# The second feed-forward product of both layers by seven products of half blocks, with sums of activations on VectorE and GpSimd, and half sums of exp on GpSimd

## The chip, the cores and the metric

The kernel runs on one core of a Trainium2 chip. The metric is the device time of one execution in microseconds. TensorE (PE) multiplies, VectorE (DVE), ScalarE (ACT) and GpSimd (POOL) do elementwise work, and SyncE (SP) issues the DMAs. Each engine works through its own instructions in order and waits on semaphores for the others. Matrix products leave their results in PSUM, of which the kernel uses eight banks of 128 x 512 fp32; everything else stands in SBUF.

## The reference

The input is `x` of 64 graphs x 256 nodes x 256 features in fp32, and `adj`, 64 x 256 x 256 integers. Two layers follow each other. The first has two graph attention steps, whose softmax is taken over the nodes; the second has eight-head attention in which the softmax weight of a pair of nodes is multiplied by one of several value projections, by the value of `adj`. Both end in the same way, and the change is in the last but one line of each:

```python
# layer 0
h = _layernorm(residual + h, g_ln1, b_ln1)
residual2 = h
ff = jnp.matmul(jax.nn.relu(jnp.matmul(h, w_ff1) + b_ff1), w_ff2) + b_ff2
return _layernorm(residual2 + ff, g_ln2, b_ln2)
# layer 1
x = _ln(src + attn_out, g1, beta1)
ff = jax.nn.gelu(x @ W1 + b1, approximate=False) @ W2 + b2
return _ln(x + ff, g2, beta2)
```

The feed-forward goes from 256 features to 1024 and back to 256. All of it is fp32.

## The kernel before

Graphs are worked on in 32 pairs. `whole_way` takes one pair through graph attention (`gat_layers`), feed-forward, attention (`attention`) and a second feed-forward, and stores it. Rows of a pair are 512: two graphs (index `b`) of 256 nodes, in two blocks of 128 (index `j`).

**How the order is made.** The kernel plans its own order while it is built. Each pair is a Python generator that yields before each step of TensorE the events that the step waits for and the PSUM banks that it needs; other engines' work is handed to `put` with an engine, an assumed duration, a rank and the events that it waits for. `run` keeps up to four pairs going, and at each moment picks the engine whose next work could begin first by these assumed times. On TensorE it takes the oldest pair of those that have been ready for 0.3 us, and otherwise the one ready first; on the others the lowest rank. `keep_order` then fixes this order for each engine. Names such as "ff", "attention" and "gat" are held by one pair at a time. So the program is a fixed interleaving of up to four pairs on each engine; at run time an instruction that is not ready holds up all that stand behind it on its engine.

**First product.** `feed_forward` already computes the first product (L689) with seven products for eight blocks (class `Blocks`, steps p1 to p7, with sums of the input blocks by `Second.add`, L360, and sums of the weights by `block_sums`, L341, once at the start). Results are copied from PSUM by ScalarE (L695), added to by VectorE (L393), and activated by ScalarE (L701), in two slabs of two 128-column slices for each half of the 1024 hidden features. The hidden activations stand transposed: `f[m]` is 128 hidden features by 512 rows.

**Second product.** For each graph block `b` and each row block `j`, eight matmuls (L720) with `f[m]` as the stationary operand and 256 columns of `w2` as the moving one add up in half a PSUM bank: 32 of 128 x 128 x 256 for each feed-forward. When a bank is full, `add_rows` (L571, VectorE) adds it to the rows `y`, already scaled by `scaled` (L604, GpSimd, two operations of 128 x 512 a graph), and `layernorm` follows: statistics on VectorE (L581, L582), the root on GpSimd (L587 to L590), the normalisation on ScalarE (L594). The first bank's additions and layernorm run while the second bank is filled. Then `transposed` (L623, and DMAs of SP) turns the rows for the next stage, except for the few `hurried` stages at both ends, which TensorE transposes.

**Attention.** For each of two graphs and two groups of four heads, `scores` (L809) fills four banks, ScalarE takes exp of them (L818), VectorE multiplies by the mask (L822, two heads at a time, 128 x 1024) and adds the two halves of the node axis (L826, 128 x 512), and `products` multiplies exp and masked exp with the values (L840) and the half sums with ones (L843). VectorE divides (L852, L853), and `into_rows` projects (L862).

Of the kernel before, what the change touches and what calls it, by code (L numbers as in the profile page):

```python
# [18 lines left out]
P = 128  # L19
# [14 lines left out]
def two_layers(ctx: ExitStack, tc: tile.TileContext, t: dict, out: bass.AP, flag: bass.AP):  # L34
# [293 lines left out]
    def first_weights(name, wide=None):  # L328
# [7 lines left out]
        return s  # L336

    def block_sums(w, there):

        for to, a, b, op in ((4, 0, 2, ALU.subtract), (2, 2, 6, ALU.add), (3, 2, 0, ALU.subtract), (5, 1, 3, ALU.subtract)):  # L340
            there = put("vector", 0.6, lambda to=to, a=a, b=b, op=op: nc.vector.tensor_tensor(w[:, to], w[:, a], w[:, b], op),  # L341
                        there, rank=5)
        return there
# [322 lines left out]
    def feed_forward(y, normal, w, func, relieved, pair, stage):  # L666

        w1, b1, w2 = w
        onwards = stage == 0
        kind = "gelu" if func == AF.Gelu else None  # L670
        half = NF // 2
        f, evacuated = [None] * NF, [[None] * NF for _ in range(2)]
        if hurried(pair, stage):
            yield from transposed_on_tensor(y, normal, stage)
        second = Second(lambda c, h: normal["yT"].rearrange("p b a (c k i) -> p c k (b a) i", c=KC, k=2)[:, c, h],
                        "sums_yT", normal[0], normal[1])

        def slabs(t):

            rows, columns = [], (slice(0, N), slice(N, 2 * N))  # L680

            def begin():
                for c in range(2):
                    rows.append(work.tile([P, 2, 512], F32, name="ff", bufs=NF // 2))
                    for n in range(2):
                        f[t + n + c * half] = rows[c][:, n]

            def multiply(to, slab, a, b, **flags):
                nc.tensor.matmul(to, lhsT=w1[:, a, (t + slab) * P:(t + slab + 1) * P], rhs=b, **flags)  # L689

            def target(c, h):
                return rows[c][:, :, columns[h]]

            def copy(c, h, event):
                return put("scalar", 0.5, lambda: nc.scalar.activation(target(c, h), blocks.bank["x"], AF.Copy), event, rank=-1)  # L695

            def activate(c, h, event, of=None):
                for n in range(2):
                    m, to = t + n + c * half, rows[c][:, n, columns[h]]
                    source = to if of is None else of[:, n]  # L700
                    evacuated[h][m] = put("scalar", 0.4, lambda m=m, to=to, source=source: nc.scalar.activation(  # L701
                        to, source, func, bias=b1[:, m:m + 1]), event, rank=h - 1, function=kind,
                        frees=["bank"] * (n and of is not None))

            first = ([normal[0], normal[1], relieved, second.there[0]], ["ff"]) if t == 0 else ([], None)
            blocks = Blocks(second, first, begin, multiply, target, copy, lambda of, event: activate(1, 0, event, of), activate)
            return blocks

        a, b = slabs(0), slabs(2)
        for step in (a.p1, b.p1, a.p2, a.p6, b.p2, b.p6, a.p5, a.p7, b.p7, b.p5, a.p4, b.p4, a.p3):  # L710
            yield from step()
        order, end = (0, 1, 4, 5, 2, 3, 6, 7), b.p3
        for b in range(2):
            for j in range(2):
                for part in (order[:half], order[half:]):
                    yield [evacuated[j][m] for m in part] if b == 0 else [], None, j == 0 and part[0] == 0
                    if j == 0 and part[0] == 0:
                        p2 = bank()
                    for m in part:
                        nc.tensor.matmul(p2[:, j * D:(j + 1) * D], lhsT=f[m][:, (2 * j + b) * P:(2 * j + b + 1) * P],  # L720
                                         rhs=w2[:, m, :], start=m == 0, stop=m == NF - 1)
                    there = took(0.43 * len(part))
                    if b == j == 0 and part[0] == 0:
                        yield from end()
                        frees_at(clock["tensor"], ["yT", "sums_yT"])
            normal[b] = layernorm(y, b, add_rows(y, p2, b, there, normal["scaled", b]))
            if onwards:
                transposed(y, normal[b], normal, b, pair, 1)
            else:
                normal[b] = scaled(y, ln[3], b, normal[b])  # L730
        done_with("ff")


    def attention(y, normal, pair, all_adj):
# [66 lines left out]
        def scores(n):  # L801
# [22 lines left out]
            def halves(q):  # L824
                h[n][q] = work.tile([P, 2, N], F32, name="h", bufs=HQ)
                nc.vector.tensor_tensor(h[n][q], a[n][q][:, :, :N], a[n][q][:, :, N:], ALU.add)  # L826

            there = [put("scalar", 0.96, lambda q=q: weight(q), there, rank=0, function="exp", needs="a", frees=["bank"] * 2)
                     for q in range(HQ // 2)]
            masked.append([put("vector", 1.14, lambda q=q: mask(q), there[q], rank=0, needs="m") for q in range(HQ // 2)] +  # L830
                          [put("vector", 0.61, lambda q=q: halves(q), there[q], rank=0, needs="h") for q in range(HQ // 2)])

# [52 lines left out]
    def layernorm_weights(g, beta, more=None):  # L885
        rows, columns, passing = [on_all(g, D), on_all(beta, D)], None, None
        if more:
            passing = work.tile([P, 2, 512], F32, name="ff", bufs=NF // 2)[:, 0, :D]
            v = t[more]
            nc.sync.dma_start(passing, bass.AP(tensor=v.tensor, offset=v.offset, ap=[[0, P], [1, D]]))  # L890
            columns = column(g + "c"), column(beta + "c")
        return *rows, Event(), columns, passing
# [3 lines left out]
    ln = [layernorm_weights("L0_gnn_g_ln1", "L0_gnn_b_ln1", "L0_gnn_b_ff2")]  # L896
    ff0 = (first_weights("L0_gnn_w_ff1p"), column("L0_gnn_b_ff1"), weights("L0_gnn_w_ff2"))
    loaded[1] = load(1, 18.0)
# [11 lines left out]
    bv, bv0 = on_all("L1_gnn_bv1", D), column("L1_gnn_bv0")  # L910
    less_bv = work.tile([P, 2, 512], F32, name="ff", bufs=NF // 2)[:, 0, :D]
    nc.sync.dma_start(less_bv, bass.AP(tensor=t["L1_gnn_bv"].tensor, offset=t["L1_gnn_bv"].offset, ap=[[0, P], [1, D]]))
    wo = weights("L1_gnn_Wo")
    ln.append(layernorm_weights("L1_gnn_g1", "L1_gnn_beta1", "L1_gnn_b2"))
    ff1 = (first_weights("L1_gnn_W1p"), column("L1_gnn_b1"), weights("L1_gnn_W2"))
    ln.append(layernorm_weights("L1_gnn_g2", "L1_gnn_beta2"))
# [37 lines left out]
    def reliefs():  # L954

        def of_feed_forward(w, gb, event):
            there = with_beta(w[1], block(w[0]), FF // 2, gb[3][1])
            put("vector", 0.0, lambda: None, block_sums(w[0], with_g(lambda at: w[0][:, at], gb[3][0], [there])), event=event)

        yield [landed["ff0"]], None, 1  # L960
# [474 lines left out]
```

## Time and profile before

| | before |
|---|---|
| median of three runs | 3079.77 us (3076.63 to 3083.66) |
| profiled execution | 3077.64 us |
| its span, first to last instruction | 3075.9 us |
| mean granted clock of TensorE | 0.994 |
| PE, PEld, DVE, ACT, POOL busy | 3010.9, 2454.7, 2234.0, 1835.1, 1032.2 us |
| second product, L720, busy | 466.4 + 461.7 us, 4096 matmul records |
| first product, L689, busy | 316.1 + 312.4 + 128.9 + 127.8 us, 3584 records |
| half sums L826 on VectorE | 185.1 us, 256 instructions |
| additions L571 on VectorE | 173.0 us, 256 instructions |

PEld is TensorE's loading of the stationary operand, which overlaps the matmuls. One fp32 `nc.tensor.matmul` of the program stands in the profile as two loads and two matmuls. Busy time is the union of the instructions' spans on an engine; a matmul's recorded span is longer than its distance to the next, since they are pipelined. A row of a group names the line, engine, operation, output and inputs and their shapes, the count, the busy time, the mean of one in ns, and after the second bar the idle time just before these instructions and what ended it.

### The profile page before, as it was taken

Reading aid. Unit: us, or ns where it says so; the run is one execution under the profiler, and the core shown is the slowest. Engines: PE = TensorE matmul, PEld = TensorE weight load, DVE = VectorE, ACT = ScalarE, POOL = GpSimd, SP = SyncE. Lnnn points to the kernel's source line nnn. Section 1 sums busy time; section 2 is a strip of 40 time slices with the busy share of each in tenths; the row PEclk is TensorE's granted clock in tenths of the full one; section 3 lists DMA queues with packets and bytes.
Section 4 is the critical chain, followed back from the end, with each engine's and each line's share of the span. In section 5 each row is a group of like instructions: output and inputs, shape, how many; then the busy total and the mean of one; then the engine's idle time right before and its main releaser. Section 6 shows DMA issues by size and latency. Waiting matters only on the chain.

```text
span 3075.9 us, 52423 instructions
## 1 busy us (share of the span) xinstructions
PE 3010.9 (98%) x19154; PEld 2454.7 (80%) x19154; DVE 2234.0 (73%) x4411; ACT 1835.1 (60%) x4186; POOL 1032.2 (34%) x1542
## 2 busy tenths in 40 slices
PE   7999999999999999999999999999999999999998
PEld 6877778877878788887888778878788778788876
DVE  5787766788776867768677676686776777767774
ACT  4556665656665566565756566565666565655654
POOL 1332244232423243232352322533325333233223
PEclk8999999999999999999999999999999999999999
DMA  6211132102321122211231122311213211121000
GB/s 181 73 51 36 56 124 79 46 28 75 109 66 50 61 76 80 73 49 56 76 99 60 42 70 69 97 66 50 66 54 96 82 53 57 62 93 58 32 1 22
DMA packets 211865, 205.76 MB, mean 67 GB/s; under 512 B 22928, under 2 KB 171280, under 8 KB 211600
## 3 DMA queue, kind: packets, MB, share of 16 engines
q1 hardware_dynamic: 211184, 202.06, 20.5%
q8 instruction: 154, 2.52, 0.3%
q14 instruction: 111, 0.91, 0.1%
q10 hardware_dynamic: 416, 0.26, 0.0%
HBM read 137.51 MB, written 64.73 MB: 66 GB/s over the span
## 4 chain that ended last, share of the span: by engine, by line
PE 79%; DVE 10%; ACT 3%; DMA 3%; POOL 2%; issue 2%; SPq 1%; DVEq 0%; POOLq 0%; ACTq 0%
PE ps L720 24%; PE ps L689 20%; PE ps L840 6%; PE ps L764 6%; PE ps L769 6%; PE ps L809 4%; PE ps L545 3%; PE ps L529 3%; PE ps L862 2%; PE ps L843 2%; DVE e L502 2%; DVE x L571 2%; DVE st L581 1%; PE ps L558 1%; DMA home<-yb 1%
## 5 line engine op out<-in xcount | busy, mean ns | idle before, releaser
L587 POOL TENSOR_SCALAR less<-mv 128x2 f32<-128x2 f32 x256 | 65.4, 255 | 1596.6 <-DVE mv L582 1561.4
L594 ACT ACTIVATE x<-x,less,rstd 128x256 f32<-128x256 f32 x512 | 279.3, 594 | 418.8 <-POOL less L590 414.9
L720 PE MATMUL ps<-w_L_gnn_w_ff,ff 128*128 128x256 f32 x2048 | 466.4, 380 | 0.0
L720 PE MATMUL ps<-w_L_gnn_W,ff 128*128 128x256 f32 x2048 | 461.7, 380 | 0.9 <-ACT ff L701 0.9
L720 PEld LDWEIGHTS ps<-w_L_gnn_W,ff 128*128 128x128 f32 x2048 | 386.9, 190 | 61.0 <-issue 5.4
L720 PEld LDWEIGHTS ps<-w_L_gnn_w_ff,ff 128*128 128x128 f32 x2048 | 387.9, 190 | 57.2 <-issue 4.3
L393 DVE TENSOR_TENSOR ff<-ps,ff 128x512 f32<-128x512 f32 x384 | 261.1, 683 | 163.6 <-PE ps L689 127.1
L822 DVE TENSOR_TENSOR m<-a,adj 128x1024 f32<-128x1024 f32 x256 | 325.4, 1271 | 20.6 <-ACT a L818 20.5
L689 PE MATMUL ps<-yT,w_L_gnn_W1p 128*128 128x256 f32 x1280 | 316.1, 384 | 10.9 <-ACT ff L695 7.4
L689 PE MATMUL ps<-yT,w_L_gnn_w_ff1p 128*128 128x256 f32 x1280 | 312.4, 384 | 12.3 <-ACT ff L695 12.3
L818 ACT ACTIVATE a<-ps 128x512 f32<-128x512 f32 x512 | 266.8, 603 | 68.0 <-PE ps L809 67.1
L689 PEld LDWEIGHTS ps<-yT,w_L_gnn_W1p 128*128 128x128 f32 x1280 | 238.3, 190 | 61.8 <-ACT ff L695 17.9
L689 PEld LDWEIGHTS ps<-yT,w_L_gnn_w_ff1p 128*128 128x128 f32 x1280 | 241.3, 191 | 56.6 <-ACT ff L695 16.7
L571 DVE TENSOR_TENSOR x<-ps,x 128x512 f32<-128x512 f32 x256 | 173.0, 680 | 152.4 <-PE ps L720 120.3
L695 ACT ACTIVATE ff<-ps 128x512 f32<-128x512 f32 x384 | 221.1, 589 | 92.0 <-PE ps L689 90.1
L604 POOL TENSOR_TENSOR x<-x,b_L_gnn_g_ln 128x512 f32<-128x512 f32 x128 | 168.7, 1318 | 274.5 <-DVE yb L623 138.3
L852 DVE RECIPROCAL h<-ps 128x256 f32<-128x256 f32 x128 | 224.1, 1752 | 49.1 <-PE ps L843 48.9
L581 DVE BATCH_NORM_STATS2 st<-x 128x6 f32<-128x256 f32 x512 | 208.4, 407 | 4.7 <-issue 0.4
L701 ACT ACTIVATE ff<-ff,c_L_gnn_b_ff 128x256 f32<-128x256 f32 x384 | 174.4, 509 | 49.4 <-DVE ff L393 48.8
L604 POOL TENSOR_TENSOR x<-x,b_L_gnn_g 128x512 f32<-128x512 f32 x128 | 166.1, 1298 | 94.4 <-ACT x L594 74.8
L589 POOL TENSOR_TENSOR rstd<-rstd,mhalf 128x2 f32<-128x2 f32 x256 | 189.1, 739 | 21.3
L701 ACT ACTIVATE ff<-ff,c_L_gnn_b 128x256 f32<-128x256 f32 x384 | 172.0, 502 | 31.6 <-DVE ff L393 31.0
(138 smaller groups left out, 5499.8 us busy)
## 6 DMA issues: line engine op xcount, KB each, us to landing
home<-yb SPq DMA_DIRECT2D x182, 256.0 KB, 2.0
yT<-home SPq DMA_DIRECT2D x728, 64.0 KB, 2.0
rows<-row SPq DMA_DIRECT2D x60, 512.0 KB, 3.8
input<-in_xT SPq DMA_DIRECT2D x32, 512.0 KB, 4.0
x<-in_x SPq DMA_DIRECT2D x32, 512.0 KB, 4.1
out<-x SPq DMA_DIRECT2D x32, 512.0 KB, 2.9
input<-in_adjT SPq DMA_DIRECT2D x30, 512.0 KB, 4.1
v<-in_adjT SPq DMA_DIRECT2D x2, 512.0 KB, 6.6
```

The costliest lines, as they stand in the source:

```text
L393: nc.vector.tensor_tensor(self.target(c, h), self.bank[bank], self.target(c, h), ALU.add)
L571: return put("vector", 0.6, lambda: nc.vector.tensor_tensor(rows, p, rows, ALU.add), *events, frees=["bank"])
L581: nc.vector.bn_stats(st[:, j, :], rows[j])
L594: nc.scalar.activation(rows[j], rows[j], AF.Identity, bias=less[:, j:j + 1], scale=rstd[:, j:j + 1])
L604: nc.gpsimd.tensor_tensor(both, both, v.rearrange("p (k d) -> p k d", k=1).to_broadcast([P, 2, D]), op)
L689: nc.tensor.matmul(to, lhsT=w1[:, a, (t + slab) * P:(t + slab + 1) * P], rhs=b, **flags)
L695: return put("scalar", 0.5, lambda: nc.scalar.activation(target(c, h), blocks.bank["x"], AF.Copy), event, rank=-1)
L701: evacuated[h][m] = put("scalar", 0.4, lambda m=m, to=to, source=source: nc.scalar.activation(to, source, func, bias=b1[:, m:m + 1]), even ...
L720: nc.tensor.matmul(p2[:, j * D:(j + 1) * D], lhsT=f[m][:, (2 * j + b) * P:(2 * j + b + 1) * P], rhs=w2[:, m, :], start=m == 0, stop=m == N ...
L818: nc.scalar.activation(a[n][q][:, k], ps[2 * q + k], AF.Exp)
L822: nc.vector.tensor_tensor(m[n][q], a[n][q], adj, ALU.mult)
L852: there = put("vector", 1.68, lambda: nc.vector.reciprocal(s, po[:, N:]), there, rank=0)
```

## The change

**Second product.** The product of a feed-forward is taken as one of 2 x 2 blocks: activations in blocks of row half `j` by hidden half `c`, `w2` in blocks of hidden half by output half. Seven block products replace eight. `last_weights` loads the four blocks of `w2` with four DMAs, `last_sums` makes three sums and replaces one block by four subtractions on VectorE at the start, and the feed-forward waits for them (`w2_there`). The activation blocks stand in four tiles of 128 x 4 x 256, with a fifth for a sum (`ff`, five buffers of 4 KB a partition instead of four of the same size). The new generator `outwards` emits, for each of seven products, eight matmuls of 128 x 128 x 128, 56 in all. Three sums of activations t1, t2, t4 are made on VectorE (128 x 1024 each) and one, t3, on GpSimd. The products 1, 6, 7 add up in one half bank "x"; 2, 5, 3 in "z" and 4 in "w" of another bank. Between them VectorE adds quarters of the result to the rows: d1, d5, d6 and d3 of 128 x 256, d24 and d7 of 128 x 512. Product 5 starts "z" anew after d24 has read it and t1 is there; 6 waits for t2 and d1, 3 for t4 and d5, 7 for t3 and d6. The layernorms of both graphs wait for d24, d3 and d7.

**Half sums.** `halves` moves from VectorE to GpSimd, at rank 1 behind the layernorm's root and t3.

**Memory.** The program is built with a DMA scratch of 1024 bytes.

```diff
+    def last_weights(name):
+
+        s = const.tile([P, 7, NF // 2, P], F32, name="w_" + name)
+        for c, h, at in ((0, 0, 0), (1, 0, 1), (1, 1, 2), (0, 1, 3)):
+            nc.sync.dma_start(s[:, at], t[name][c * FF // 2:(c + 1) * FF // 2, h * P:(h + 1) * P].rearrange("(k p) d -> p k d", p=P))
+        return s
+
+    def last_sums(w, there, event):
+        for to, a, b in ((4, 3, 0), (5, 2, 4), (6, 2, 3), (3, 1, 5)):
+            there = put("vector", 0.6, lambda to=to, a=a, b=b: nc.vector.tensor_tensor(w[:, to], w[:, a], w[:, b], ALU.subtract),
+                        there, rank=5, event=event if to == 3 else None)
...
-        order, end = (0, 1, 4, 5, 2, 3, 6, 7), b.p3
-        for b in range(2):
-            for j in range(2):
-                for part in (order[:half], order[half:]):
-                    yield [evacuated[j][m] for m in part] if b == 0 else [], None, j == 0 and part[0] == 0
-                    if j == 0 and part[0] == 0:
-                        p2 = bank()
-                    for m in part:
-                        nc.tensor.matmul(p2[:, j * D:(j + 1) * D], lhsT=f[m][:, (2 * j + b) * P:(2 * j + b + 1) * P],
-                                         rhs=w2[:, m, :], start=m == 0, stop=m == NF - 1)
-                    there = took(0.43 * len(part))
-                    if b == j == 0 and part[0] == 0:
-                        yield from end()
-                        frees_at(clock["tensor"], ["yT", "sums_yT"])
-            normal[b] = layernorm(y, b, add_rows(y, p2, b, there, normal["scaled", b]))
+        yield from outwards(y, normal, f, evacuated, w2, w2_there, b.p3)
+        for g in range(2):
+            normal[g] = layernorm(y, g, *normal["added"])
...
+        def product(n, to, side, first=False):
+            for b in range(2):
+                for k in range(half):
+                    nc.tensor.matmul(banks[to][:, b], lhsT=side[:, k, b * P:(b + 1) * P], rhs=w2[:, n - 1, k],
+                                     start=first and b == k == 0, stop=True, skip_group_check=True)
+            return took(1.8)
+
+        def add(to, of, us, *events, frees=()):
+            return put("vector", us, lambda: nc.vector.tensor_tensor(to, of, to, ALU.add), *events,
+                       *(normal["scaled", b] for b in range(2)), rank=-1, frees=frees)
+
+        def combine(to, a, b, op, *events, engine="vector", us=1.14):
+            return put(engine, us, lambda: getattr(nc, engine).tensor_tensor(to, a, b, op), *events, rank=0)
...
+        yield [w2_there, *done(0, 0)], None, 1
+        x = banks["x"] = bank()[:, :D].rearrange("p (b d) -> p b d", b=2)
+        read1 = product(1, "x", a11, True)
+        d1 = add(quarter(0, 0), x, 0.34, read1)
+        yield from end()
+        frees_at(clock["tensor"], ["yT", "sums_yT"])
+        s1 = work.tile([P, half, N], F32, name="ff", bufs=5)
+        t1 = combine(s1, a21, a22, ALU.add, *done(1, 0), *done(1, 1))
+        t3 = combine(a21, a11, a21, ALU.subtract, *done(0, 0), t1, engine="gpsimd", us=2.5)
+        yield done(0, 1), None, 1
+        both = bank().rearrange("p (j b d) -> p j b d", j=2, b=2)
+        banks["z"], banks["w"] = both[:, 0], both[:, 1]
+        read2 = product(2, "z", a12, True)
+        yield done(1, 1), None, 0
+        there = product(4, "w", a22)
+        d24 = add(rows[:, :, :, :P], both, 0.6, read2, there)
+        t2 = combine(a11, s1, a11, ALU.subtract, t3, read1)
+        t4 = combine(a12, a12, a11, ALU.subtract, t2, read2)
+        yield [t1, d24], None, 0
+        d5 = add(quarter(1, 1), banks["z"], 0.34, product(5, "z", s1, True))
+        yield [t2, d1], None, 0
+        d6 = add(quarter(0, 1), x, 0.34, product(6, "x", a11))
+        yield [t4, d5], None, 0
+        d3 = add(quarter(0, 1), banks["z"], 0.34, product(3, "z", a12), frees=["bank"])
+        yield [t3, d6], None, 0
+        d7 = add(rows[:, 1].rearrange("p b (h d) -> p b h d", h=2),
+                 x.rearrange("p b (h d) -> p b h d", h=1).to_broadcast([P, 2, 2, P]), 0.6, product(7, "x", a21), d5, frees=["bank"])
+        normal["added"] = [d24, d3, d7]
...
-                nc.vector.tensor_tensor(h[n][q], a[n][q][:, :, :N], a[n][q][:, :, N:], ALU.add)
+                nc.gpsimd.tensor_tensor(h[n][q], a[n][q][:, :, :N], a[n][q][:, :, N:], ALU.add)
...
-                          [put("vector", 0.61, lambda q=q: halves(q), there[q], rank=0, needs="h") for q in range(HQ // 2)])
+                          [put("gpsimd", 1.35, lambda q=q: halves(q), there[q], rank=1, needs="h") for q in range(HQ // 2)])
...
-    nc = bacc.Bacc("TRN2", target_bir_lowering=False, num_devices=1)
+    nc = bacc.Bacc("TRN2", target_bir_lowering=False, num_devices=1, dynamic_dma_scratch_size=1024)
```

## The prediction

> **What bounds the kernel now.** I read the page's busy shares first, then its groups, then the waits of PE, then two stretches of the timeline for prices, and last the busy times of consecutive 8 us windows.
>
> ```profile
> PE 3010.9 (98%) x19154; PEld 2454.7 (80%) x19154; DVE 2234.0 (73%) x4411; ACT 1835.1 (60%) x4186; POOL 1032.2 (34%) x1542
> L720 PE MATMUL ps<-w_L_gnn_w_ff,ff 128*128 128x256 f32 x2048 | 466.4, 380 | 0.0
> L720 PE MATMUL ps<-w_L_gnn_W,ff 128*128 128x256 f32 x2048 | 461.7, 380 | 0.9 <-ACT ff L701 0.9
> L822 DVE TENSOR_TENSOR m<-a,adj 128x1024 f32<-128x1024 f32 x256 | 325.4, 1271 | 20.6 <-ACT a L818 20.5
> L571 DVE TENSOR_TENSOR x<-ps,x 128x512 f32<-128x512 f32 x256 | 173.0, 680 | 152.4 <-PE ps L720 120.3
> L604 POOL TENSOR_TENSOR x<-x,b_L_gnn_g_ln 128x512 f32<-128x512 f32 x128 | 168.7, 1318 | 274.5 <-DVE yb L623 138.3
> ```
>
> PE is the bound: 98% busy, and the second product (L720) has next to no idle time before it. The reader should note where the slack is: L571, the only VectorE work of L720, waits for PE and never makes PE wait. PE's waits say the same; L720 is in them with one wait of 0.9 us:
>
> ```profile
> PE ps L689 <- ACT ff L695: 23.5, 31, 1.7
> PE ps L558 <- ACT xw L510: 11.6, 2, 10.6
> PE ps L720 <- ACT ff L701: 0.9, 1, 0.9
> ```
>
> The timeline gives pitches. (Start, us, engine, line, count; each 128x256 fp32 product is two matmul records.)
>
> ```profile
> 18.23 1.06 PE L465 MATMUL ps<-ident,rise 128*128 128x128 f32 x8 [0.90 <-ACT rise L452]
> 19.02 2.76 PEld L933 LDWEIGHTS ps<-c_L_gnn_b_ln1c,w_L_gnn_w_ff1p 128*128 128x128 f32 x24
> ...
> 3054.81 8.37 PE L720 MATMUL ps<-w_L_gnn_W,ff 128*128 128x256 f32 x38
> ```
>
> L720: (8.37-0.38)/37 = 0.216 us per record at 256 columns. At 128 columns (L465) it is (1.06-0.27)/7 = 0.113; weight loads alone (L933, moving one column) follow each other at (2.76-0.19)/23 = 0.112. So one load hides behind 256 columns, and just about balances 128.
>
> The windows (PE, PEld, DVE, ACT, POOL busy of 8 us) show where VectorE is full:
>
> ```profile
> 1410.00:1418.00 8.00, 8.00 (x49) 6.57 (x48) 8.00 (x12) 6.29 (x12) 0.00 (x0) 1.00 0.30 107
> 1418.00:1426.00 8.00, 8.00 (x98) 5.35 (x97) 7.68 (x17) 4.85 (x11) 0.00 (x0) 1.00 0.00 0
> ...
> 1442.00:1450.00 8.00, 8.00 (x98) 5.35 (x96) 7.52 (x18) 1.82 (x4) 0.00 (x0) 1.00 0.01 2
> 1450.00:1458.00 8.00, 8.00 (x38) 7.07 (x38) 7.55 (x18) 2.78 (x10) 2.51 (x8) 1.00 0.00 0
> ```
>
> In attention VectorE is 94 to 100% busy with GpSimd idle, and PE stays full because L720 is filler that asks VectorE for little.
>
> **The Trainium skill.** *TensorE: Matmul & The Clock Gate*, LDWEIGHTS: a load takes its columns / 1.2 GHz, 107 ns for 128; the trace's 112 ns agrees. *SBUF — State Buffer*, "SBUF: two separate sides": a GpSimd operation and a VectorE operation with two SBUF inputs exclude each other for a whole instruction. The trace agrees: a half sum (0.69 us alone) that meets a GpSimd one takes 1.76, and the GpSimd one 2.15 instead of 1.27:
>
> ```profile
> 160.23 1.18 DVE L822 TENSOR_TENSOR m<-a,adj 128x1024 f32<-128x1024 f32 x1
> 161.33 1.76 DVE L826 TENSOR_TENSOR h<-a 128x512 f32<-128x512 f32 x1
> ...
> 160.39 2.15 POOL L604 TENSOR_TENSOR x<-x,b_L_gnn_g_ln 128x512 f32<-128x512 f32 x1 [6.73 <-DVE yb L623]
> ```
>
> **The change, part by part.** There are 64 feed-forwards, two for each of 32 pairs.
>
> *PE.* 64 records a feed-forward at 0.216 (13.8 us) become 7 x 8 x 2 = 112 of 128 columns. I take 0.110 (bounds 0.109, the 128 columns at L720's rate, and 0.113): 12.3 us. Saved 1.5 us each, 96 us in all (75 to 102). PE is the bound, so this counts whole, less new waits.
>
> *VectorE.* Gone: two L571 additions a feed-forward (128 x 0.68 = 87) and 256 half sums (mean 0.723, 185). New: 256 quarter additions at 0.41 (L853, PSUM, 256 elements: 105), 128 of 0.68 (87), 192 sums of 128x1024 at 1.22 (a mask that meets nobody: 234). Net +154 us, to 2388, before port waits. *GpSimd.* 256 half sums at 1.27 (325) and 64 differences of 128x1024, which no trace row shows: *GPSIMD Engine Reference*, 2.1, gives some 2.5 cycles an element, 2.13 us at 1.2 GHz, and the same rule plus 0.2 fits the row of 512 elements (1.27), so an estimate of 2.34 (150). GpSimd goes from 1032 to about 1507 us. Half sum and mask are released by the same exp and hold the same port, so moving one to the other engine saves VectorE little: 4 masks and 4 half sums were 4 x (1.22+0.69) = 7.6 us in turn on VectorE, and are 4 x (1.22+1.27) = 10 us in turn on the port, less what VectorE does from PSUM meanwhile.
>
> *New waits of PE.* Before, the products of L720 had only to wait for activations. Now product 5 writes into the PSUM half that products 2 and 4 shared the bank with: it waits for d24, the addition that reads both. In the order of the changed kernel's instructions, product 5 comes directly behind product 4 in 52 of 64 feed-forwards. Price: product 4's last record is about 0.27 (L465), VectorE starts 0.04 later, d24 0.68, PE restarts 0.05 later: 1.04 instead of one pitch of 0.11, and where PE had to stop its second record came at 0.32 instead of 0.216 (L689), so 1.03 us if VectorE is idle just then. VectorE will be 80% busy and is in order; with masks of 1.22 and sums ahead of d24 I add 0.5 (0 to 1.5). 52 x 1.5 = 78 us (54 to 130).
>
> Product 6 is directly behind product 5 in 40. It needs the chain t1 (VectorE 1.22), t3 (GpSimd 2.34, queued behind half sums of 1.27), t2 (1.22 on VectorE, in order, behind masks): 4.8 us alone, covered by products 4 and 5 and some activation lead. I take 1.3 us (0.3 to 3), 52 us. Products 3 and 7 have a covering product each: 10 us (0 to 30).
>
> The attention products wait for masks and half sums; in the trace of before the first of them starts a median of 1.2 us after the last. In the window where they meet t1 and t3 the port must give 4 x 2.49 + 1.22 + 2.34 = 13.5 us while PE has about 9 us of other work. Against this, PE has then just stood still for product 5. I take 0.4 us for each of 64: 26 us (0 to 120). VectorE blocked by the port also holds up the additions of the first product queued behind it (L393); inside these bounds.
>
> *Hidden or small.* Eight differences of weights at the start (8 x 0.69 on VectorE at the lowest rank, four smaller loads for each large one on SP's queue, same bytes): hidden by the first pairs' work, 2 us (0 to 5). At the end nothing covers: both graphs are normalised only after product 7, so a second graph's statistics (1.2) and GpSimd scaling (2.5) lie behind the last matmul, and products 5 and 6 stand bare: 6 us. Scaling (4 x 1.3 = 5.2 us on GpSimd) is now needed by d1, at the first product instead of the end; the first product's 12 us of PE lie before it, so nothing, but up to 20 us if GpSimd is more than 6 us behind. The smaller DMA scratch: no GpSimd-issued DMA in the page, nothing.
>
> Sum: -96 + 78 + 52 + 10 + 26 + 8 = +78, less a few us of old waits that vanish as PE falls behind (L689's 23 us; I take 6): +72. The profiled execution took 3077.64 us (span 3075.9), 2 under the median of the three runs, 3079.77. So 3079.8 + 72, about 3152.
>
> **Rivals.**
> *A. PE saving wins (faster).* If d24 always finds VectorE idle (54 us), product 6 is nearly always ready (12) and the attention products' lead absorbs the port (0), then -100 + 54 + 12 + 8: about 3054. It decides below 96 us of new waits. For it: GpSimd is idle in exactly the full windows. Against: product 5's turnaround costs half the gain even so.
> *B. The port becomes the limit in attention.* GpSimd 1507 and VectorE's two-input work (masks 312, L360 about 160, L500 and L502 about 250, new sums 234: 956) make 2463 us on one port, 80%, and more than all of the time in the attention windows. If each pair of attention products stalls 1.5 us instead of 0.4, that is 70 more: about 3222.
> *C. A 128-column pair does not overlap its load* (0.190, the load's recorded time, as pitch): 7168 x 0.19 = 1362 instead of 884, about 3600. L465 and L933 speak against it. The reverse, that the products gain nothing (0.123), gives about 3250 with the waits above.
>
> **How the numbers follow.** My case, slower by 1 to 4% through product 5 and 6: 0.63. B: 0.19. A: 0.10. Between A and mine, within 0.2% (about what a measurement of this kernel can tell from no change): 0.05. C: 0.03. Faster: A and no more, 0.10; same 0.05; slower 0.85. My case's own range is 3090 to 3200; the range for 8 in 10 reaches into A's neighbourhood and over B: 3065 to 3250.
>
> **What will show it.** Right: PE's share falls to about 94%; a new wait of PE's second product on the addition of both graphs' halves, some 50 times and 1 to 2 us each; another on the sums, some 30 to 40 times; the second product's own busy time near 800 us; masks with a mean over 1.4 us; GpSimd near 1500 us. Wrong: no such waits (then A), or PE waits mostly of the attention products (then B), or a pitch well over 0.113 at 128 columns (then C).

## The result, and the profile after

The changed kernel takes 3359.26 us (median of four runs, 3356.68 to 3364.66) against 3080.20 us, a ratio of 1.0908 with a 95% interval of 1.0889 to 1.0928: 279 us slower. The prediction said slower, 3152 us with a range up to 3250. The direction was right; the loss was almost four times as large as forecast. The profiled execution took 3364.66 us, its span is 3362.9 us, and the mean granted clock of TensorE fell from 0.994 to 0.964.

From the page after (busy shares, then groups: busy time, mean ns, idle time before):

```profile
PE 3036.7 (90%) x22226; PEld 2566.5 (76%) x22226; DVE 2656.6 (79%) x4611; ACT 1823.1 (54%) x4184; POOL 1723.9 (51%) x1862
...
L885 POOL TENSOR_TENSOR h<-a 128x512 f32<-128x512 f32 x256 | 485.7, 1918 | 255.9 <-ACT a L877 255.9
L747 PE MATMUL ps<-w_L_gnn_W,ff 128*128 128x128 f32 x3584 | 474.0, 291 | 118.2 <-DVE ff L756 68.2
...
L747 PE MATMUL ps<-w_L_gnn_w_ff,ff 128*128 128x128 f32 x3584 | 472.3, 290 | 95.6 <-DVE x L752 79.4
...
L881 DVE TENSOR_TENSOR m<-a,adj 128x1024 f32<-128x1024 f32 x256 | 455.3, 1796 | 18.7 <-ACT a L877 18.6
...
L756 DVE TENSOR_TENSOR ff<-ff 128x1024 f32<-128x1024 f32 x192 | 305.7, 1592 | 21.8 <-POOL ff L756 17.7
...
L756 POOL TENSOR_TENSOR ff<-ff 128x1024 f32<-128x1024 f32 x64 | 153.3, 2396 | 168.5 <-DVE ff L756 162.3
```

The second product (L747, before L720) had 0.9 us of idle time in front of it and now has 213.8. No elementwise engine is full over the whole span. The masks (L881) went from 1.27 to 1.80 us, the half sums take 1.92 us on GpSimd, and the sums on VectorE 1.59 us in the mean, although the shortest of them takes 1.18 and the median one 1.22: some meet an operation of GpSimd and most do not.

PE's waits after (total us, times, longest us):

```profile
PE ps L747 <- DVE x L752: 129.1, 73, 3.4
PE ps L747 <- DVE ff L756: 84.2, 34, 5.3
PE ps L921 <- DVE qk L912: 26.0, 16, 3.3
PE ps L557 <- ACT xw L522: 24.1, 8, 4.2
PE ps L697 <- ACT ff L703: 20.4, 20, 1.7
```

L752 are the additions d1 to d7, L756 the sums t1 to t4. By the trace, 57 of the 73 waits on L752, 121.9 us of them, end with the addition of 128 x 512, d24; these are product 5 waiting, 2.14 us each. The other 16 (7.1 us) are product 3 waiting for d5. Of the waits on L756, 33 (84.1 us) are product 6 waiting for t2.

In these 57 cases d24 starts 1.56 us after product 4's end in the mean. Most of that time VectorE is in a sum: t1 in 40 of the 57, 46.8 us of some 89; the sums of the first product's input (L372) take 14.0 and masks 7.5.

One stretch shows both waits and the clock after them. These are consecutive windows of 3.41 us (columns: PE, PEld, DVE, ACT, POOL busy with counts, then the granted clock of PE, DMA share, GB/s):

```profile
717.68:721.10 3.42, 3.42 (x37) 2.85 (x35) 3.42 (x4) 3.37 (x5) 1.80 (x2) 1.00 0.47 131
721.10:724.51 3.41, 0.78 (x7) 0.69 (x7) 3.41 (x4) 3.22 (x7) 1.26 (x1) 1.00 0.05 10
724.51:727.92 3.41, 2.49 (x13) 2.19 (x11) 3.41 (x2) 0.00 (x0) 3.41 (x3) 0.50 0.00 0
727.92:731.34 3.42, 0.19 (x1) 0.20 (x2) 3.42 (x4) 0.00 (x0) 2.09 (x1) 0.50 0.00 0
731.34:734.75 3.41, 3.41 (x16) 3.29 (x16) 1.89 (x4) 0.00 (x0) 0.00 (x0) 0.50 0.00 0
734.75:738.16 3.41, 3.41 (x65) 2.04 (x68) 1.31 (x2) 0.00 (x0) 0.00 (x0) 1.00 0.00 0
```

And its timeline (start, duration in us, engine, line):

```profile
719.14 2.05 PE L747 MATMUL ps<-w_L_gnn_W,ff 128*128 128x128 f32 x16
723.82 3.17 PE L747 MATMUL ps<-w_L_gnn_W,ff 128*128 128x128 f32 x16 [2.63 <-DVE x L752]
731.15 3.76 PE L747 MATMUL ps<-w_L_gnn_W,ff 128*128 128x128 f32 x16 [4.15 <-DVE ff L756]
...
720.82 1.21 DVE L881 TENSOR_TENSOR m<-a,adj 128x1024 f32<-128x1024 f32 x1
721.96 1.21 DVE L756 TENSOR_TENSOR ff<-ff 128x1024 f32<-128x1024 f32 x1
723.09 0.68 DVE L752 TENSOR_TENSOR x<-ps,x 128x512 f32<-128x512 f32 x1
723.69 5.20 DVE L881 TENSOR_TENSOR m<-a,adj 128x1024 f32<-128x1024 f32 x2
728.81 0.41 DVE L752 TENSOR_TENSOR x<-ps,x 128x256 f32<-128x256 f32 x1
729.15 1.95 DVE L756 TENSOR_TENSOR ff<-ff 128x1024 f32<-128x1024 f32 x1
...
723.25 2.36 POOL L756 TENSOR_TENSOR ff<-ff 128x1024 f32<-128x1024 f32 x1 [3.77 <-DVE ff L756]
725.57 4.44 POOL L885 TENSOR_TENSOR h<-a 128x512 f32<-128x512 f32 x2
```

Product 4 ends at 721.2. VectorE is in a mask and has t1 queued ahead of d24, so d24 starts at 723.09 and product 5 at 723.82, after 2.63 us. Meanwhile t3 runs on GpSimd until 725.61, and the two masks behind d24, 1.21 us when alone, together take 5.20 us beside t3 and the half sums. Only then come d5 and t2 (which itself takes 1.95 us), and product 6 starts at 731.15, after another stand of 4.15 us. From 724.51 to 734.75 TensorE's granted clock is 0.50: product 5's 16 records take 3.17 us and product 6's 3.76, where product 4's took 2.05.

So the trace's span can be split in three. *Stands* are the time up to the last matmul in which none is in progress, some 7 us before the first one included. *Half clock* is half of the time in which matmuls ran at a granted clock of 0.50: records of L747 follow each other at 0.213 us there (median) and at 0.112 at a clock of 1.00. *Rest* is what is left of the span: TensorE's work as it would be at full clock, and the 12 to 15 us after the last matmul.

| | span | stands | half clock | rest |
|---|---|---|---|---|
| before | 3075.9 | 52.4 | 9.7 | 3013.8 |
| after | 3362.9 | 311.6 | 96.8 | 2954.5 |
| difference | +287.0 | +259.2 | +87.1 | -59.3 |

The change does save work of TensorE: start to start the records of 128 columns follow each other at 0.112 us, those of 256 at 0.216. It pays for this more than five times over, three quarters of it in stands and one quarter in work done at half clock after the stands.

### The profile page after: what moved, and what is told of

Its sections match the earlier page's. It is cut to its first block, busy times and chain, and to the rows that moved or that the text cites. A ratio compares the mean times of both kernels' runs of the same rounds, so it can differ in the third digit from the quotient of the medians.

```text
span 3362.9 us, 59156 instructions
## 1 busy us (share of the span) xinstructions
PE 3036.7 (90%) x22226; PEld 2566.5 (76%) x22226; DVE 2656.6 (79%) x4611; ACT 1823.1 (54%) x4184; POOL 1723.9 (51%) x1862
## 4 chain that ended last, share of the span: by engine, by line
PE 54%; DVE 32%; ACT 4%; DMA 3%; issue 3%; POOL 2%; SPq 1%; DVEq 0%; ACTq 0%; POOLq 0%
PE ps L697 15%; PE ps L747 13%; DVE m L881 8%; DVE ff L756 6%; PE ps L823 6%; PE ps L828 5%; PE ps L899 5%; PE ps L868 3%; DVE ff L405 2%; DVE sums_yT L372 2%; DVE x L752 2%; PE ps L921 2%; DVE e L514 2%; DVE e L512 2%; DVE h L911 2%
## 5 line engine op out<-in xcount | busy, mean ns | idle before, releaser
L885 POOL TENSOR_TENSOR h<-a 128x512 f32<-128x512 f32 x256 | 485.7, 1918 | 255.9 <-ACT a L877 255.9
L747 PE MATMUL ps<-w_L_gnn_W,ff 128*128 128x128 f32 x3584 | 474.0, 291 | 118.2 <-DVE ff L756 68.2
L599 POOL TENSOR_SCALAR less<-mv 128x2 f32<-128x2 f32 x256 | 60.8, 238 | 1004.7 <-DVE mv L594 993.9
L747 PEld LDWEIGHTS ps<-w_L_gnn_W,ff 128*128 128x128 f32 x3584 | 455.4, 204 | 146.9 <-DVE ff L756 74.7
L747 PE MATMUL ps<-w_L_gnn_w_ff,ff 128*128 128x128 f32 x3584 | 472.3, 290 | 95.6 <-DVE x L752 79.4
L747 PEld LDWEIGHTS ps<-w_L_gnn_w_ff,ff 128*128 128x128 f32 x3584 | 456.0, 204 | 121.0 <-DVE x L752 85.7
L881 DVE TENSOR_TENSOR m<-a,adj 128x1024 f32<-128x1024 f32 x256 | 455.3, 1796 | 18.7 <-ACT a L877 18.6
L752 DVE TENSOR_TENSOR x<-ps,x 128x256 f32<-128x256 f32 (+1 forms) x384 | 193.1, 504 | 236.8 <-PE ps L747 235.6
L756 DVE TENSOR_TENSOR ff<-ff 128x1024 f32<-128x1024 f32 x192 | 305.7, 1592 | 21.8 <-POOL ff L756 17.7
L697 PEld LDWEIGHTS ps<-yT,w_L_gnn_W1p 128*128 128x128 f32 x1280 | 236.8, 190 | 65.8 <-ACT ff L703 26.9
L756 POOL TENSOR_TENSOR ff<-ff 128x1024 f32<-128x1024 f32 x64 | 153.3, 2396 | 168.5 <-DVE ff L756 162.3
L533 ACT ACTIVATE xw<-ps 128x260 f32<-128x260 f32 (+1 forms) x256 | 95.1, 388 | 218.8 <-PE ps L541 157.3
```

Of the source, the lines that this page charges most:

```text
L747: nc.tensor.matmul(banks[to][:, b], lhsT=side[:, k, b * P:(b + 1) * P], rhs=w2[:, n - 1, k], start=first and b == k == 0, stop=True, skip_ ...
L752: return put("vector", us, lambda: nc.vector.tensor_tensor(to, of, to, ALU.add), *events, *(normal["scaled", b] for b in range(2)), rank=- ...
L756: return put(engine, us, lambda: getattr(nc, engine).tensor_tensor(to, a, b, op), *events, rank=0)
L881: nc.vector.tensor_tensor(m[n][q], a[n][q], adj, ALU.mult)
L885: nc.gpsimd.tensor_tensor(h[n][q], a[n][q][:, :, :N], a[n][q][:, :, N:], ALU.add)
```

## The experiments

Theory at the outset: two kinds of stand, of product 5 on d24 and of products 6 and 3 on the sums, each worsened by VectorE and GpSimd holding each other up, and the half clock as their consequence. Rivals: that the half sums on GpSimd are the larger cause, that the two waits are one delay which can be booked under either line, and that the half clock comes with the small products themselves. All of the runs, with the same split; the ratio is to the kernel before on the same chip.

| kernel | us | ratio (95%) | stands | half clock | rest |
|---|---|---|---|---|---|
| half sums only | 3103.11 | 1.0074 (1.0057 to 1.0091) | 66.9 | 16.3 | 3019.8 |
| products only | 3294.05 | 1.0695 (1.0677 to 1.0712) | 267.5 | 60.8 | 2966.9 |
| own bank | 3375.56 | 1.0958 (1.0940 to 1.0976) | 306.3 | 112.2 | 2962.9 |
| t3 on VectorE | 3263.25 | 1.0596 (1.0578 to 1.0613) | 229.4 | 74.0 | 2962.7 |
| all on VectorE | 3249.23 | 1.0556 (1.0537 to 1.0575) | 228.6 | 61.6 | 2956.3 |
| all on VectorE, own bank | 3238.68 | 1.0518 (1.0499 to 1.0537) | 210.6 | 64.5 | 2959.2 |
| the same, measured costs | 3205.76 | 1.0423 (1.0406 to 1.0441) | 187.6 | 49.3 | 2960.1 |
| measured costs alone | 3311.32 | 1.0760 (1.0730 to 1.0790) | 267.2 | 91.8 | 2953.2 |
| filler | 3372.21 | 1.0943 (1.0923 to 1.0962) | 235.4 | 69.9 | 3067.1 |
| no sums | 3193.87 | 1.0378 (1.0353 to 1.0403) | 188.5 | 52.5 | 2946.0 |
| no sums, own bank | 3090.95 | 1.0047 (1.0030 to 1.0065) | 111.7 | 14.2 | 2956.6 |
| no sums, own bank, half sums on VectorE | 3056.53 | 0.9935 (0.9918 to 0.9951) | 89.8 | 27.1 | 2937.2 |

The last column is the check on the split: it is 3014 and 3020 with eight products, and 2937 to 2967 in all kernels with seven and no added work, whatever their time. Nearly all that differs between those lies in the two columns before it.

### One part at a time

Half sums on GpSimd in the kernel before:

```diff
-                nc.vector.tensor_tensor(h[n][q], a[n][q][:, :, :N], a[n][q][:, :, N:], ALU.add)
+                nc.gpsimd.tensor_tensor(h[n][q], a[n][q][:, :, :N], a[n][q][:, :, N:], ALU.add)
```

> The kernel before with one edit: half sums on GpSimd, the second product as it was. Theory T (the seven products' new waits and the half clock behind them make the loss; the port only lengthens them): masks go from 1.27 to about 1.7 us and half sums to about 1.8, but PE's waits grow little, 3080 to 3120 us, clock still 0.99. Rival R1 (the half sums on GpSimd are the culprit, through the shared port): most of the loss is here, 3230 us or more.

The seven products, with the half sums left on VectorE (the reverse of this diff, in the changed kernel):

> The changed kernel with the half sums back on VectorE, at its old cost and rank. T: the waits on the additions and sums of the second product stay, with VectorE even fuller (about 2640 us busy): 3280 to 3380 us, clock about 0.965. R1: the loss is gone with the half sums, 3050 to 3130 us, clock above 0.985.

The half sums alone cost 23 us, the products alone 214, both together 279: some 42 us come only from the two together. In the groups of the kernel with half sums alone:

```profile
L826 POOL TENSOR_TENSOR h<-a 128x512 f32<-128x512 f32 x256 | 465.3, 1836 | 482.4 <-ACT a L818 482.4
...
L822 DVE TENSOR_TENSOR m<-a,adj 128x1024 f32<-128x1024 f32 x256 | 428.8, 1692 | 13.1 <-ACT a L818 13.1
```

The half sum is 1.84 us instead of the 1.27 that the prediction took from the trace of before, and the mask 1.69 instead of 1.27. VectorE gave away 185 us of half sums and got 103 back in longer masks (428.8 against 325.4). With L720 still there to fill in, that cost only 23 us. The products alone have, in PE's waits:

```profile
PE ps L747 <- DVE ff L756: 79.5, 49, 4.0
PE ps L747 <- DVE x L752: 61.5, 40, 3.8
PE ps L697 <- ACT ff L703: 53.7, 42, 2.9
PE ps L921 <- DVE qk L912: 33.7, 18, 2.6
```

Both new waits are there without the half sums on GpSimd. The rival that these are the larger cause falls.

### Taking one wait away

Product 5 in a bank of its own, so that it no longer waits for d24:

```diff
-        d24 = add(rows[:, :, :, :P], both, 0.6, read2, there)
+        d24 = add(rows[:, :, :, :P], both, 0.6, read2, there, frees=["bank"])
...
-        yield [t1, d24], None, 0
+        yield [t1], None, 1
+        banks["z"] = bank()[:, :D].rearrange("p (b d) -> p b d", b=2)
```

> The changed kernel, where product 5 gets a bank of its own and waits for t1 alone, no longer for d24. T: the wait of product 5 on the addition (129 us with the others on these additions) falls below 60 us, and some of the half clock with it: 3200 to 3280 us, clock about 0.975. Rival R2 (VectorE and the port are simply late, so product 5 or 6 waits the same time for the sums): waits on additions turn into waits on sums, 3330 us or more.

PE's waits then:

```profile
PE ps L747 <- DVE ff L756: 186.3, 88, 5.9
PE ps L922 <- DVE qk L913: 43.4, 22, 3.4
...
PE ps L747 <- DVE x L752: 3.5, 7, 0.5
```

The wait on d24 is gone (the waits on additions fall from 129.1 to 3.5 us), those on the sums have grown from 84.2 to 186.3, and the time did not fall; it rose by 16 us. My theory was wrong here and the rival right: with the changed kernel's other parts in place, product 5 merely moves up to the next thing that VectorE owes it, t1 (40 waits, 65.8 us by the trace), and product 6 to t2 (41 waits, 119.4 us). TensorE stands as long as before, 306 us against 312.

### Relieving the port

t3 alone moved to VectorE, and then also the half sums:

```diff
-        t3 = combine(a21, a11, a21, ALU.subtract, *done(0, 0), t1, engine="gpsimd", us=2.5)
+        t3 = combine(a21, a11, a21, ALU.subtract, *done(0, 0), t1, us=1.14)
```

> The changed kernel with the difference t3 on VectorE (1.2 us) instead of GpSimd (2.4 us). T: the chain t1, t3, t2 is shorter by over 1 us and blocks the port less, VectorE is fuller by 78 us; PE's wait on sums (84 us) falls by a third to a half, that on additions stays: 3310 to 3350 us. R2 (VectorE's load decides): slower than the changed kernel, 3370 us or more.

> The changed kernel with all four sums of activations and the half sums on VectorE, so that the change brings GpSimd no work. Theory Q (the port's blocking makes VectorE late): masks back to about 1.3 us, VectorE's busy time no higher than the 2657 us of the changed kernel although it does 400 us more work; 3180 to 3240 us. Rival V (VectorE's amount of work makes the waits): 3290 us or more, as the kernel with only the half sums put back, 3294.

Moving t3 alone leaves

```profile
PE ps L747 <- DVE x L752: 112.6, 45, 4.9
PE ps L747 <- DVE ff L756: 35.0, 19, 3.4
```

and with the half sums moved as well the masks are at

```profile
L881 DVE TENSOR_TENSOR m<-a,adj 128x1024 f32<-128x1024 f32 x256 | 356.4, 1392 | 5.0 <-ACT a L877 4.6
```

Moving t3 gains 96 us, more than expected: stands fall from 312 to 229 us, those on the sums from 84 to 35. With the half sums moved as well, VectorE is busier than in the changed kernel (2699 against 2657 us, where theory Q had no increase) and the kernel is still 110 us faster than that. So GpSimd's help cost more than it gave: t3 takes 2.40 us there instead of 1.2, with t2 behind it, and it holds up VectorE for that time. The Trainium skill (*SBUF — State Buffer*, "SBUF: two separate sides") says of the shared port that whoever starts first has it for the whole instruction; the masks bear it out, with 1.80 us in the changed kernel and 1.39 with nothing of the change on GpSimd. But 229 us of stands remain with nothing of the change on GpSimd, so the port is not the whole cause. The second time is 9 us above the upper end of theory Q; rival V, that VectorE's amount of work alone decides, falls.

### Adding work instead of taking waits away

Four unread 128 x 128 x 128 products are put behind product 4 and four behind product 5. Nothing else is moved.

```diff
+        def fill():
+            for k in range(half):
+                nc.tensor.matmul(whole[:, D:D + P], lhsT=w2[:, 0, k % half], rhs=w2[:, 1, k % half],
+                                 start=False, stop=True, skip_group_check=True)
...
         there = product(4, "w", a22)
+        fill()
```

> The changed kernel in the same order, with four matmuls of 128x128x128 that nobody reads behind product 4 and again behind product 5 of each feed-forward: 115 us of PE work more. Theory C (PE stands there anyway, and the standing brings the clock to half for 122 us of loss): PE's recorded waits fall by about 80 to 100 us, the clock rises from 0.964 to 0.975 or more, time 3300 to 3365 us although 115 us of work are added. Rival (the waits aren't there for the fill to take, or the clock doesn't follow them): 3420 us or more.

These are 1024 records at 0.112, 115 us of work, and the rest column has grown by 113. The time grew by 13 us, a little above the forecast: stands fell by 76 and the half clock by 27. PE's waits:

```profile
PE ps L747 <- DVE ff L756: 71.1, 28, 4.4
PE ps L747 <- DVE x L752: 68.7, 51, 2.4
```

This is the direct measurement of what a missing filler costs. TensorE had nothing to do in these places, and work put there is nearly free; some of it is paid back in clock. It also answers the third rival: with 1024 more small records the half clock cost less, not more. The traces say the same: in the twelve kernels with seven products, 482 of the 3.41 us windows at full clock are filled by L747 almost alone (over 3.2 us of it, under 0.2 us of stands), and none was followed by half clock.

### Without the sums

All four sums are left out; products 3, 5, 6 and 7 take unsummed blocks.

```diff
-        t1 = combine(s1, a21, a22, ALU.add, *done(1, 0), *done(1, 1))
-        t3 = combine(a21, a11, a21, ALU.subtract, *done(0, 0), t1, engine="gpsimd", us=2.5)
...
-        d5 = add(quarter(1, 1), banks["z"], 0.34, product(5, "z", s1, True))
+        d5 = add(quarter(1, 1), banks["z"], 0.34, product(5, "z", a21, True))
```

> The changed kernel without the four sums of activations: products 3, 5, 6 and 7 take unsummed blocks, so the second product isn't that of the reference. All matmuls, the quarter additions and the half sums on GpSimd stay. T: without the sums (192 on VectorE, 64 on GpSimd) the waits fall to those on the additions, 30 to 80 us, and the saving of PE, 84 us, shows: 3040 to 3130 us, clock above 0.985. Rival (the waits on the additions, d24 first, are the larger part): 3200 us or more.

```profile
PE ps L747 <- DVE x L752: 108.7, 61, 3.7
PE ps L697 <- ACT ff L703: 24.9, 24, 1.9
```

The time lies above the theory's and just under the rival's. Without any sum, and with VectorE at 2340 us instead of 2657, the wait on the additions still costs 108.7 us, and 60 of its 61 times are d24, where the changed kernel had 57. The prediction had priced one such turn at 1.03 us with VectorE idle; in a queue with masks of 1.59 us it is 1.8.

Then with product 5 in its own bank too, and then with the half sums on VectorE as well, so that only the seven products and their additions stay of the change:

> The changed kernel without the four sums (products 3, 5, 6 and 7 take unsummed blocks of the activation, so the result is not the reference's) and with product 5 in a bank of its own: both of TensorE's new waits are gone, while the seven products, their records of 128 columns and VectorE's half sums stay as the change has them. Without the sums alone the time was 3194 us. Theory C (the two waits and the half clock that follows them are the whole loss): TensorE's gaps in front of the second product fall to 15 us or less, the granted clock is 0.985 or more and the time 3020 to 3090 us, about or below the kernel before (the shorter product is worth 84 us, the half sums on GpSimd cost 23). Rival D (VectorE's additional accumulations d24 and d1 to d7 delay it wherever they are waited for): the waits move to other lines, the clock stays at 0.982 or less and the time at 3150 us or more.

> The changed kernel without the four sums (products 3, 5, 6 and 7 take unsummed blocks, so the result is not the reference's), with product 5 in a bank of its own and with the half sums back on VectorE: what stays of the change is the seven products in records of 128 columns and their accumulations. With the half sums on GpSimd this was 3091 us, with 112 us of gaps in front of TensorE (52 before the change), 56 us of them in the first product behind late evacuations on VectorE and ScalarE. Theory G (the half sums on GpSimd are what is left: they hold VectorE's masks up): the masks fall from 1.71 to about 1.35 us, the gaps to 60 to 80 us and the time to 3010 to 3055 us, so that the shorter product shows its 84 us in part or whole. Rival A (the additional accumulations of VectorE are what is left): the time stays at 3075 us or above.

The first of these has, in PE's waits,

```profile
PE ps L697 <- DVE ff L405: 27.6, 14, 3.4
PE ps L697 <- ACT ff L703: 22.2, 28, 1.6
...
PE ps L747 <- DVE x L752: 2.3, 3, 1.3
```

and the second

```profile
L882 DVE TENSOR_TENSOR m<-a,adj 128x1024 f32<-128x1024 f32 x256 | 344.2, 1344 | 9.5 <-ACT a L878 9.4
```

With both waits gone nearly all of the loss is gone: 3091 us, just over the forecast's upper end. This shows that two waits which in part take each other's place had to be removed together: leaving out the sums alone gave 165 us, the bank alone nothing, both 268. Leaving out the sums also takes their work from VectorE and GpSimd, so these runs do not tell waiting for a sum apart from the load that the sum is. With masks of 1.34 us in place of 1.71, as theory G has it, the time falls by another 34 us to 3056.53, just over its forecast (so are the stands, 89.8 us). That is 0.65% below the kernel before (0.5 to 0.8%), and all that the shorter product is worth when none of its sums has to be made. What this kernel keeps of the change besides (the weights in seven blocks, the fifth buffer, the smaller DMA scratch) is therefore not where the 279 us come from.

### Both remedies with the sums kept

The edits for "all on VectorE" (t3 and half sums) and for the own bank together:

> The changed kernel with all four sums and the half sums on VectorE (nothing of the change left on GpSimd, so the two engines no longer hold each other up over it) and with product 5 in a bank of its own, so that it does not wait for the evacuation d24. With the sums on VectorE alone the time was 3249 us, TensorE's waits on the sums 52.5 us and on d24 96.3 us. Theory T (two waits, each of them real once the other is gone): the waits on d24 fall below 10 us, those on the sums rise to 60 to 100 us, TensorE's gaps fall from 229 to 150 to 190 us and the time to 3150 to 3230 us. Rival M (VectorE's turnaround is one cost that only changes the line it is booked under): the waits on the sums take over all of it, 130 us or more, and the time stays at 3240 us or above.

```profile
PE ps L747 <- DVE ff L756: 118.8, 67, 4.1
```

It takes 3238.68 us, 11 us less than without the bank, and its waits on the sums are 118.8 us where that had 52.5. The stands, 210.6 us, missed theory T's 150 to 190; this is close to rival M's picture, 1 us under its limit of 3240 (the waits on the sums stay 11 us under its 130). Giving VectorE all of the sums does not make the two waits separable.

Next the planner was told, in the changed kernel, durations as its trace has them:

```diff
-        def combine(to, a, b, op, *events, engine="vector", us=1.14):
+        def combine(to, a, b, op, *events, engine="vector", us=1.6):
...
-            masked.append([put("vector", 1.14, lambda q=q: mask(q), there[q], rank=0, needs="m") for q in range(HQ // 2)] +
-                          [put("gpsimd", 1.35, lambda q=q: halves(q), there[q], rank=1, needs="h") for q in range(HQ // 2)])
+            masked.append([put("vector", 1.75, lambda q=q: mask(q), there[q], rank=0, needs="m") for q in range(HQ // 2)] +
+                          [put("gpsimd", 1.9, lambda q=q: halves(q), there[q], rank=1, needs="h") for q in range(HQ // 2)])
```

> The changed kernel, planned with the durations that its own profile shows: masks 1.75 us, half sums 1.9, sums of activations 1.6. Theory P (the order was laid out for a VectorE and a GpSimd that don't block each other; with true durations other work is put in the gaps): PE's waits on the second product fall to about half, 3180 to 3260 us. Rival S (in any order VectorE and the port are late in the attention windows, there is no free work to put in): 3320 us or more.

And all three together, with 1.40, 1.39 and 0.84 us in these places, all on VectorE:

> The changed kernel with all sums and half sums on VectorE, product 5 in a bank of its own (3239 us so far), and the planner told what these operations take in the trace: 1.40 us for a sum, 1.39 for a mask and 0.84 for a half sum in place of 1.14, 1.14 and 0.61. If the waits on the sums are there because the planner believes them to be ready too early, it puts other work in front and the time falls to 3130 to 3190 us; if VectorE has no room left in the stretches where the sums are due (it is busy 83% of the span), it stays at 3220 us or above.

Knowing the durations is worth 48 us in the changed kernel and 33 us in the last one, and both end between their two forecasts. In the changed kernel that is 3311 us, over theory P's 3260 and much nearer to rival S: the waits on the second product did not halve, and the stands only fell from 312 to 267. The order is part of the cause, then, and by these two runs a small one. In the last kernel the largest wait is

```profile
PE ps L747 <- DVE ff L756: 95.9, 51, 5.2
```

and nothing is left on d24. At 3205.76 us it is the fastest of those that keep the sums; none came near the kernel before.

## Why the prediction was right in direction and wrong in size

Two steps of the sum failed. The new waits were priced with operations that meet nobody, plus 0.5 us for the queue, so that the stands were put at 168 us and measured 259. And the clock was put at nothing and cost 87 us.

**What bounds the kernel, and the two waits.** Right. The product that waited for nothing was the filler, and the change made it wait. d24 was read from the order: 52 places forecast, 57 waits measured. The sums: about 40 forecast, 34 measured. The port effect was seen in the right place.

**Term "product 5", 78 us.** The mechanism held, the size did not: 57 waits of 2.14 us, 121.9 us. The step that failed is "I add 0.5" for masks and sums ahead of d24: the queue adds about 1.1, and more than half of the time that VectorE lets d24 wait is t1, not masks. The result lies inside the term's bounds of 54 to 130.

**Terms "product 6" and "products 3 and 7", 62 us.** Products 3 and 7 cost 7 us where 10 were forecast. Product 6 cost 84.1 where 52 were: 2.5 us for each of 33, not 1.3 for each of 40. The chain t1, t3, t2 was priced with operations that meet nobody (1.22 and 2.34) and ran with sums of 1.59 and masks of 1.80 in between.

**Durations.** VectorE was put at 2388 us before port waits and took 2657, GpSimd at 1507 and took 1724. Half sums cost 1.92 us each, not 1.27; masks over 1.4 were forecast, and came at 1.80. t3, estimated at 2.34 from the Trainium skill (*GPSIMD Engine Reference*, 2.1), measured 2.40.

**Term "attention products", 26 us.** Wrong in place. The attention products waited for nothing in the changed kernel. What waits is the projection behind them (L921, 26.0 us) for VectorE's divisions, and a product of the first graph attention step (L557, L545 before) for ScalarE, 24.1 us where before it was 4.0. That one of these also comes to 26 us is chance. Rival B, which would have shown at the attention products, did not occur.

**Term "PE", -96 us.** The pitch of 0.112 was near the assumed 0.110: 7168 x 0.112 - 4096 x 0.216 = -82. But the rest column fell by only 59, and by 77 in the kernel that waits least. Some 9 of the missing 23 us are the second records after stands, 86 of which came at about 0.213 instead of 0.112 although the clock was full; the others stay open. Rival C is excluded by the pitch; with the waits above, its own sum would have come to about 3730 and not 3600. The sign "the second product's own busy time near 800" was badly chosen: busy time joins the overlapping recorded spans and came to 946, of which a part was run at half clock; only the start-to-start distance shows the pitch.

**The term that was missing.** The sum took a stand to cost its own length. It also costs the clock: 87.1 us more of half clock, more than the forecast's whole loss of 72. The prediction showed the clock's column in its windows, at 1.00 throughout, and never asked what would happen to it when PE's share fell, to 94% by its forecast and to 90% as measured.

Forecast and measurement of the span differ by 287 - 72 = 215 us: 91 because the stands were 259 and not 168 (78 + 52 + 10 + 26 + 8 - 6), 87 for the clock, and 37 because TensorE's work shrank by 59 and not 96. Of the 91, product 5 makes 44, product 6 makes 32, and most of the rest lies outside the second product. The start and end, put at 8 us, weren't measured by themselves.

**Separable terms.** The sum added d24's wait and the sums' wait as if each could be taken away by itself. The experiments show that removing one gives back nothing (own bank) or leaves the other nearly as large (no sums: 108.7 us). Both are VectorE being late for the same few products.

## What to carry to other kernels

Work that waits for nothing is what hides the other stages' elementwise work; a cheaper version that needs an engine's answer in its middle loses that use first, and its saving has to be set against the stands of everything it used to cover. When two waits on the same engine follow each other closely, price them together, by the time at which the engine can be done with both, and test by removing both. And a stand of TensorE of about 2 us is to be priced with the half clock that follows it.

## What the runs showed of the hardware

The granted clock moves in steps of 3.41 us and takes the values 1.00 and 0.50 in these traces. I compared PE's stands in each such window with the clock of the next one. In the changed kernel 858 windows stayed at full clock, and none of them had more than 1.89 us of stands; 47 were followed by half clock, and all but two had over 1.95 us, each time in a single stand. The two, at 52.1 and 99.9 us, had 0.46 and 0 us of stands, but 2.15 and 2.95 us of the matmuls of one moving column with which the biases are prepared (L992). All other runs but the one with the filler have such windows too, between 51 and 163 us and nowhere else. So a TensorE that is busy by the profile is not always enough to keep the clock. Apart from these, windows of the other runs stayed at full clock with up to 1.96 us of stands, and the least that was followed by half clock was 1.69. At half clock, windows with over 0.71 us of stands never led back to full in any of the runs. So the stand of 2.63 us in the windows shown above, within one of them, was enough to halve the clock, and the next stand kept it there for three. The Trainium skill (*TensorE: Matmul & The Clock Gate*, "HAM oscillation — how this bites in real kernels") has the half rate and a window of 3.4 us, which these traces confirm; its rule of no idle gaps over about 3.4 us is too lenient here: only 20 stands of the changed kernel were that long, and it fell to half clock 45 times after stands. Whether several short stands that add up to 2 us do the same, the runs don't settle.

The port's exclusion has a price even at modest load: GpSimd 51% and VectorE 79% busy, and the half sums still took 1.92 us against 1.27 assumed and the masks 1.80 against 1.27.
